# Gates of four batches computed further ahead inside a recurrence, with smaller weight buffers

## The chip, the cores and the metric

The kernel runs on one core of one Trainium2 chip. The metric is the device time of one execution in microseconds (us); lower is better. All data and matmuls are float32.

## The reference, cut to what matters

Input x has 16 batches, 512 time steps and 512 features. Four layers follow one another, each added to its input: x = x + layer(x).

```
L0: x1 = x + (x + gated wavelet)       -> the kernel uses x1 = x * (2 + gate)
L1: h_t = tanh(x1_t @ Wx + b + h_(t-1) @ Wh),  x2 = x1 + h          (512 steps, one after the other)
L2: f = sigmoid(x2 @ Wf + bf); i = sigmoid(x2 @ Wi + bi)
    s = f + i + eps;  f = f / s;  i = i / s * (x2 @ Wc + bc)
    out = scans over time of f and i;   x3 = x2 + out
L3: layer_b = base + A_b @ B_b^T  (A_b, B_b of rank 8, from cond);  out = x3 + x3 @ layer_b
```

The gates f and i and the candidate of L2 at step t need only x2 at that step. The scans need all steps.

## The kernel before, in words

There are two parts. The first is the recurrence L1: 64 blocks (index n) of T = 8 steps (index s). The order of the instructions on PE, ACT, DVE and SP is written out by hand there (a manual schedule), so program order is queue order. Features lie on partitions in four chunks of 128 (KC = 4).

In each step PE first does the recurrent matmuls (line 459, issued by `accumulate`, L320; 16 of them, four side by side in array columns of 32), from the state h of the step before. Then come other matmuls that don't depend on this step: `inputs` (L333, again through L320) of the next block, as many calls as `SHARE` (L435) says, two a step, four matmuls each; in steps 4 to 7 of blocks 0 to 16 one `factor_part` (L292), which makes the rank-8 factors of L3 from its weights; and from step 128 on one call of `early_gate` (L337, matmuls L352). Then ACT does four tanh (L485) and DVE four transposes (L486), which give the next state. In half of the steps DVE then adds x1 and h to x2 (L491), in the others it makes x1 of a later block (L158). After that `do_jobs` (L501) issues work that `later` has put off to this step. At the end of steps 7, 0 and 2 `begin` (L412) copies the bias into a bank of the next block or the one after (L428, on ACT).

`early_gate` makes L2's gates for the first TE = 128 steps of all batches. A unit is one gate (f, i or candidate) of one output chunk j of two batches: 256 columns, four calls (one for each input chunk k). After the fourth, ACT takes a sigmoid (L377), DVE does the sum (L394), the reciprocal in four parts (L380), two products (L383, L399) and the candidate (L387), spread over the next steps by `later`, and f and i are stored to the DRAM tile `early` (L374). The PSUM banks of these units alternate between `pf` and `pg`, each of one buffer; `pf` is also the bank of `factor_part`. The tiles of f, i and s are taken from the tag `w2` of six buffers of 128 x 512, which is also that of L3's weights: `load_chunks` (L257) and `load_factor` (L273) load two of a factor's four weight chunks in step 1 and two in step 6 of the block before the one that uses them. `store_factor` (L301) writes the factor to DRAM at the block's end, in four stores. After blocks 2 to 9 two chunks of the gate weights or of `base` are loaded (L512 to L516), the four matrices in turn.

All loads and stores are issued by the queue of SP, in program order.

The second part goes through the batches b (L618). `gate_unit` (L539) does one output chunk j: 12 matmuls for the steps from TE on (L544), sigmoids (L559), loads of the early gates (L558), on DVE a sum, reciprocal (L561), products and three scans (L569, L573, L575), on POOL two sums that give x3 (L578, L579). `make_layer` (L593) makes layer_b. `last_layer` (L605) of batch b runs after the second unit of batch b + 1, with 16 matmuls (L610), copies by ACT (L614) and stores (L615); for the last two batches it runs at the very end. The banks `pf`, `pi` have one buffer, `pc` two; tiles f, i, s and the output tiles two.

## Time and profile before

| | us |
|---|---|
| median of three runs (1655.62 to 1656.74) | 1656.73 |
| the profiled execution | 1657.68 |
| its span, first to last instruction | 1655.8 |
| PE busy (98% of the span) | 1627.2 |
| DVE busy (68%) | 1125.6 |
| ACT busy | 426.4 |
| POOL busy | 207.0 |

First tanh of block 8 at 131.67, of block 16 at 238.59, of block 17 at 253.63, last step at 910.79. The first gate matmul of the second part starts at 912.13.

Times in the lines shown later are microseconds from the start of the span. A line of the timeline holds start, duration, engine, source line, operation, what it writes and reads, shapes and count, and in brackets the time for which the engine was idle before it, and what ended that. PE is TensorE's matmuls, PEld its weight loads, SPq the issue of a transfer. A line of the chain of waits holds start, duration, engine and line. A line of the groups holds, after the first bar, busy time in us and mean ns of one. One matmul call of float32 appears as two records.

### The profile page before, as it was taken

What the parts mean: (1) busy time and instruction counts of PE and PEld (TensorE: products, weight loads), DVE (VectorE), ACT (ScalarE), POOL (GpSimd) and SP (SyncE); (2) the same over time, 40 slices, a digit from 0 to 9 for tenths busy, and PEclk for the clock granted to TensorE, in tenths of its full rate; (3) what the DMA queues carried; (4) which work ended last, traced back from release to release, by engine and by line L of the source; (5) the groups of instructions that cost most, each with busy time, mean ns of one, the idle gap of its engine ahead of it and who ended that gap; (6) DMA issues with size and microseconds to landing.
All of it is one profiled execution on the core that took longest, in us unless ns stands there. A gap on an engine that the chain in (4) does not pass through costs nothing.

```text
span 1655.8 us, 70230 instructions
## 1 busy us (share of the span) xinstructions
PE 1627.2 (98%) x30501; PEld 1176.0 (71%) x30501; DVE 1125.6 (68%) x3557; ACT 426.4 (26%) x2507; POOL 207.0 (12%) x209
## 2 busy tenths in 40 slices
PE   7999999999999999999999999999999999999998
PEld 6888888888888888888888555555555555555553
DVE  3445545555565555555555888889888888888985
ACT  3333333333333333333333111111111111111111
POOL 0000000000000000000000322233232222232321
PEclk9999999999999999999999999999999999999999
DMA  6344331111111111111110011110101111111001
GB/s 197 114 144 152 113 94 30 33 37 36 36 36 35 34 37 36 36 37 36 36 36 17 27 37 41 39 40 21 38 33 39 39 38 41 37 40 40 24 29 54
DMA packets 100805, 83.60 MB, mean 50 GB/s; under 512 B 10880, under 2 KB 78976, under 8 KB 100496
## 3 DMA queue, kind: packets, MB, share of 16 engines
q1 hardware_dynamic: 99392, 79.02, 15.3%
q8 instruction: 239, 3.92, 1.0%
q14 instruction: 70, 0.57, 0.1%
q10 hardware_dynamic: 1104, 0.08, 0.0%
HBM read 53.38 MB, written 25.69 MB: 48 GB/s over the span
## 4 chain that ended last, share of the span: by engine, by line
PE 93%; DVE 4%; issue 1%; ACT 1%; DMA 0%; SPq 0%; POOLq 0%; POOL 0%; DVEq 0%; ACTq 0%
PE pre L320 40%; PE po L610 12%; PE pg L352 10%; PE pf L544 9%; PE pi L544 9%; PE pc L544 9%; DVE h_out L486 1%; DVE s L561 1%; PE pl L600 1%; ACT a L485 1%; PE pf L292 1%; DVE s L569 0%; DMA w_sb<-in_w1T_dram 0%; DVE s L573 0%; DVE i L572 0%
## 5 line engine op out<-in xcount | busy, mean ns | idle before, releaser
L320 PE MATMUL pre<-wh_sb,h_out 128*32 128x128 f32 x16384 | 547.6, 273 | 10.2 <-DVE h_out L486 1.5
L320 PEld LDWEIGHTS pre<-wh_sb,h_out 128*32 128x32 f32 x16384 | 454.7, 109 | 107.4 <-DVE h_out L486 101.8
L486 DVE STREAM_TRANSPOSE h_out<-a 128x32 f32<-128x32 f32 x2048 | 262.1, 185 | 359.4 <-ACT a L485 358.4
L485 ACT ACTIVATE a<-pre 128x32 f32<-128x32 f32 x2048 | 238.2, 202 | 566.9 <-PE pre L320 564.9
L320 PE MATMUL pre<-wx_sb,x 128*32 128x128 f32 x8192 | 320.9, 273 | 1.3 <-issue 1.2
L320 PEld LDWEIGHTS pre<-wx_sb,x 128*32 128x32 f32 x8192 | 235.6, 110 | 6.9 <-ACT pre L428 4.2
L610 PE MATMUL po<-layer,x 128*128 128x512 f32 x480 | 208.4, 592 | 0.0
L544 PE MATMUL pf<-x,wf_sb 128*128 128x384 f32 x512 | 177.3, 489 | 1.0 <-DVE x L491 1.0
L544 PE MATMUL pc<-x,wc_sb 128*128 128x384 f32 x512 | 175.6, 486 | 0.0
L544 PE MATMUL pi<-x,wi_sb 128*128 128x384 f32 x512 | 175.6, 486 | 0.0
L610 PEld LDWEIGHTS po<-layer,x 128*128 128x128 f32 x480 | 91.2, 190 | 111.6 <-issue 107.6
L561 DVE RECIPROCAL s<-s 128x384 f32<-128x384 f32 x64 | 163.4, 2553 | 2.2
L544 PEld LDWEIGHTS pf<-x,wf_sb 128*128 128x128 f32 x512 | 95.9, 190 | 79.9 <-issue 18.1
L544 PEld LDWEIGHTS pi<-x,wi_sb 128*128 128x128 f32 x512 | 97.3, 190 | 67.8
L544 PEld LDWEIGHTS pc<-x,wc_sb 128*128 128x128 f32 x512 | 97.3, 190 | 67.8
L578 POOL TENSOR_TENSOR s<-s,f 128x512 f32<-128x512 f32 x64 | 87.6, 1368 | 387.4 <-DVE s L573 375.2
L491 DVE TENSOR_TENSOR x<-x,h_out 128x128 f32<-128x128 f32 x256 | 101.1, 395 | 31.9 <-PE pg L352 2.9
L533 POOL MEMSET zero<- 128x1 f32 x1 | 0.1, 99 | 912.9 <-DMA early<-ei 912.9
L559 ACT ACTIVATE f<-pf,vec_sb 128x384 f32<-128x384 f32 x64 | 37.3, 582 | 275.2 <-POOL s L578 115.0
L614 ACT COPY osb<-po 128x512 f32<-128x512 f32 x64 | 37.5, 586 | 266.2 <-PE po L610 170.0
L560 DVE SCALAR_TENSOR_TENSOR s<-f,i 128x384 f32<-128x384 f32 x64 | 36.7, 573 | 100.3 <-ACT i L559 100.3
L579 POOL TENSOR_TENSOR x<-s,x 128x512 f32<-128x512 f32 x64 | 81.4, 1272 | 5.0
(82 smaller groups left out, 1271.7 us busy)
## 6 DMA issues: line engine op xcount, KB each, us to landing
xb<-in_xT_dram SPq DMA_DIRECT2D x64, 256.0 KB
w<-in_l3w_dram SPq DMA_DIRECT2D x64, 256.0 KB
out_dram<-osb SPq DMA_DIRECT2D x64, 256.0 KB
early<-ef SPq DMA_DIRECT2D x32, 128.0 KB
early<-ei SPq DMA_DIRECT2D x32, 128.0 KB
f<-early SPq DMA_DIRECT2D x64, 64.0 KB
i<-early SPq DMA_DIRECT2D x64, 64.0 KB
w_sb<-in_w1T_dram SPq DMA_DIRECT2D x1, 1024.0 KB
```

The costliest lines, as they stand in the source:

```text
L320: nc.tensor.matmul(pre[PLACE[g][0]][j * BP : (j + 1) * BP, PLACE[g][1], :], lhsT, tile_columns(w, j), start=False, stop=False, skip_group_ ...
L352: nc.tensor.matmul(ps[c * BP : (c + 1) * BP, :, :], w[:, k, j * P + c * BP : j * P + (c + 1) * BP], x2[:, k, pair, :TE], start=(k == 0), s ...
L485: nc.scalar.activation(a[:, at], pre[bank][:, place, at], AF.Tanh)
L486: nc.vector.transpose(turned[:, c, :], a[:, at])
L491: nc.vector.tensor_tensor(x2[:, :, :, at].rearrange("p k b t -> p k t b"), xs[n][:, :, t0 // 2, :, :], turned.rearrange("p k (t b) -> p k ...
L544: nc.tensor.matmul(p[:, TE:], w_sb[:, k, j * P : (j + 1) * P], x2[:, k, b, TE:], start=(k == 0), stop=(k == KC - 1),)
L559: nc.scalar.activation(gate[:, new], p[:, new], AF.Sigmoid, bias=col(bias, j))
L561: nc.vector.reciprocal(s[:, new], s[:, new])
L578: nc.gpsimd.tensor_tensor(s, s, f, ALU.add)
L579: nc.gpsimd.tensor_tensor(x3[:, j, :], s, x2[:, j, b, :], ALU.add)
L610: nc.tensor.matmul(po, x3[:, k, at], layer[:, k, :], start=(k == 0), stop=(k == KC - 1))
L614: nc.scalar.copy(osb, po)
```

## The change

`early_gate` works on a list of parts, `PARTS`, each with its batches and steps, in place of pairs of batches with the steps 0 to 127. The list is: batches 12 to 15, steps 0 to 63; the six pairs of batches 0 to 11, steps 0 to 127; batches 12 to 15, steps 64 to 127, then 128 to 191. Each part has 256 columns. The first part's 48 calls are made in steps 64 to 127 (blocks 8 to 15), in the steps s of `SLOTS` of each block; the others from step 128 on, one a step, as before. In blocks 8 to 15 `SHARE` moves calls of `inputs`. The units of the first part, and one after it, use the bank `pg` alone; in that part the candidate is first copied by ACT with its bias to a tile `ec`. The tiles ef, ei, es, ec have one buffer each of 128 x 256. L3's weights have four buffers in place of six; a factor's first two chunks are loaded in step 6 of the block before its use, the other two in step 0 of the block that uses them, with the loads of its bias. The gate weights come matrix by matrix. In the second part, batches 12 to 15 compute the steps from 192 on and load 192.

```diff
-TE = 128
+FIRST, MAIN = 64, 128
+SLOTS = (0, 2, 4, 5, 6, 7)
+QUAD = slice(12, 16)
+PARTS = [(QUAD, slice(0, 64))]
+PARTS += [(slice(b, b + 2), slice(0, 128)) for b in range(0, 12, 2)]
+PARTS += [(QUAD, slice(64, 128)), (QUAD, slice(128, 192))]
+TE = 192
...
-            tiles.append(w2pool.tile([P, D], F32, tag="w2", name=f"{name}_{k}", bufs=6))
+            tiles.append(w2pool.tile([P, D], F32, tag="w2", name=f"{name}_{k}", bufs=4))
...
-        b, j = divmod(group, KC)
-        pair = slice(2 * b, 2 * b + 2)
+        part, j = divmod(group, KC)
+        batches, steps = PARTS[part]
+        shape = [P, batches.stop - batches.start, steps.stop - steps.start]
+        first = part == 0
+        single = first or u == 3 * KC
         if k == 0:
-            pool, tag = ((ps_p, "pf"), (ps_q, "pg"))[u % 2 if u else 1]
+            pool, tag = ((ps_p, "pf"), (ps_q, "pg"))[1 if single else u % 2]
...
-                x2[:, k, pair, :TE],
+                x2[:, k, batches, steps],
...
             early_gate.tiles = [
-                w2pool.tile([P, D], F32, tag="w2", name=f"{name}_{group}", bufs=6)[:, : 2 * TE].rearrange(
-                    "p (b t) -> p b t", b=2
-                )
-                for name in ("ef", "ei", "es")
+                w2pool.tile(shape, F32, tag=tag, name=f"{tag}_{group}") for tag in ("ef", "ei", "es", "ec")
             ]
...
-            nc.sync.dma_start(out=early[pair, which, j].rearrange("b p t -> p b t"), in_=got)
+            nc.sync.dma_start(out=early[batches, which, j, :, steps].rearrange("b p t -> p b t"), in_=got)
...
+            if first:
+                nc.vector.tensor_tensor(i, i, candidate, ALU.mult)
+            else:
+                nc.vector.scalar_tensor_tensor(i, ps, col(C_BH, j), i, ALU.add, ALU.mult)
...
+        now = early_gate.step
         if which == 0:
-            later(q if u == 0 else q + 2, lambda: sigmoid(f, C_BF))
+            later(now if single else now + 2, lambda: activate(f, AF.Sigmoid, C_BF))
...
-            later(q + 4, times_candidate)
+            if first:
+                later(now, lambda: activate(candidate, AF.Identity, C_BH))
+            later(now + (3 if first else 4), times_candidate)
...
+    SHARE = [[(2 * s, 2 * s + 2) for s in range(T)] for _ in range(NBLK)]
+    SHARE[0] = (0, 0), (0, 0), (0, 0), (0, 3), (3, 7), (7, 10), (10, 13), (13, 16)
+    for n in range(FIRST // T, MAIN // T):
+        SHARE[n] = (0, 2), (2, 6), (6, 8), (8, 12), (12, 13), (13, 14), (14, 15), (15, 16)
...
-            if n < 2 * R and s in (1, KC + 2):
-                coming = load_factor(n, coming, range(KC // 2) if s == 1 else range(KC // 2, KC))
+            if n < 2 * R and s == KC + 2:
+                coming = load_factor(n, None, range(KC // 2))
+            if 0 < n <= 2 * R and s == 0:
+                loaded = load_factor(n - 1, loaded, range(KC // 2, KC))
...
-            q = n * T + s - TE
-            if q >= 0:
-                early_gate(q)
+            step = n * T + s
+            if step >= MAIN or step >= FIRST and s in SLOTS:
+                early_gate.step = step
+                early_gate(made)
+                made += 1
...
-                k, which = divmod(i, 4)
+                which, k = divmod(i, KC)
...
+        te = TE if b in range(B)[QUAD] else MAIN
...
-                    p[:, TE:],
+                    p[:, te:],
...
-                    x2[:, k, b, TE:],
+                    x2[:, k, b, te:],
...
-        old, new = slice(0, TE), slice(TE, S)
+        old, new = slice(0, te), slice(te, S)
...
-            nc.sync.dma_start(out=gate[:, old], in_=early[b, which, j])
+            nc.sync.dma_start(out=gate[:, old], in_=early[b, which, j, :, old])
```

## The prediction

> **What bounds the kernel now.** I read the mean clock first (0.999, so no throttling to explain), then the busy slices, the timeline of single steps of the recurrence, the groups, and last the chain of waits of the end. A block is 8 steps of the recurrence, a step is the time from one first tanh (L485) to the next, a piece is one call of early_gate (4 matmuls of 256 columns).

> Blocks 1 to 15 have no gate work. One step of block 10, from the timeline:

> ```profile
> 161.09 0.65 PE L320 MATMUL pre<-wx_sb,x 128*32 128x128 f32 x16
> 161.34 0.47 ACT L485 ACTIVATE a<-pre 128x32 f32<-128x32 f32 x4 [1.18 <-PE pre L320]
> 161.57 0.59 DVE L486 STREAM_TRANSPOSE h_out<-a 128x32 f32<-128x32 f32 x4 [0.98 <-ACT a L485]
> 161.83 0.81 PEld L320 LDWEIGHTS pre<-wh_sb,h_out 128*32 128x32 f32 x32 [0.37 <-DVE h_out L486]
> 162.98 0.47 ACT L485 ACTIVATE a<-pre 128x32 f32<-128x32 f32 x4 [1.01 <-PE pre L320]
> ```

> The loop is closed: recurrent matmuls, tanh, transpose, next recurrent matmuls. Its tanhs come 1.64 us apart, and the last bracket of PEld shows 0.37 us in which PE waits for the transpose. The steps with factor matmuls (165.12 to 169.58) have the same 1.645. So the steps are bound by latency, with PE not filled. From step 128 on it is otherwise:

> ```profile
> 302.45 0.46 PEld L320 LDWEIGHTS pre<-wx_sb,x 128*32 128x32 f32 x16
> 302.80 0.47 ACT L485 ACTIVATE a<-pre 128x32 f32<-128x32 f32 x4 [1.28 <-PE pre L320]
> 302.88 0.24 PEld L352 LDWEIGHTS pg<-x,wf_sb 128*32 128x32 f32 x8
> 303.30 0.91 PEld L320 LDWEIGHTS pre<-wh_sb,h_out 128*32 128x32 f32 x32 [0.17 <-DVE h_out L486]
> 304.19 0.46 PEld L320 LDWEIGHTS pre<-wx_sb,x 128*32 128x32 f32 x16
> ```

> Weight loads start at 302.45, 302.88, 303.30, 304.19: inputs take 0.43, the gate piece 0.42, the recurrent part 0.89, together 1.74. PE is the bound here, and a step is 1.742 (301.06, 302.80, 304.55). With factor matmuls (0.22) as well, steps of block 16 are 1.96 apart (247.75, 249.71, 251.67, 253.63).

> In the second part (from 912) PE runs 24 gate records of one unit at 0.322 us each (2.575 per 8), and one batch takes 45.96 us (one reciprocal at 1543.13, the same one a batch later at 1589.10). DVE needs 9.13 us for one unit (1543.13, 1552.27, 1561.40) and idles 7.15 us a batch: PE is the bound until the last batches. There the chain of waits changes engine:

> ```profile
> 1571.31 2.58 PE pf L544 x8
> 1573.89 2.59 PE pi L544 x8
> 1576.51 0.59 ACT i L559
> 1577.19 0.57 DVE s L560
> ...
> 1634.13 1.20 DVE f L575
> ...
> 1636.53 1.26 POOL s L578
> ...
> 1639.18 13.14 PE po L610 x26
> ```

> From 1577.19 to 1636.4 the end hangs on DVE alone (six units), then POOL, while PE idles 2.6 us before the last layer.

> [...]after the idle at 1636.6 the granted clock is 0.50 from 1639.95 for 3.4 us. [...]this trace has 0.322 us at 384 and 0.431 at 512 columns, 0.85 ns a column and record, and that decides. [...]sigmoids at 256 columns 475 to 499 ns.[...]

> **Part 1, the first pieces (steps 64 to 127).** 48 pieces enter, six a block. PE per new step: steps 0 and 2: 0.89 + 0.43 + 0.42; steps 1 and 3: recurrent 0.87 and four input calls 0.87; steps 4 to 7: 0.87 + 0.22 + 0.22 + 0.43. Each is 1.74; the moved inputs make them even. 64 x (1.742 - 1.645) = +6.2 us: of 20.6 us of new matmuls (48 x 0.43) some 14 go into PE time that is idle today. The ACT sigmoids and Identity (0.5 us) run after the gate ends, 1.05 us after the recurrent part, and finish by 1.53; the next tanh is due at 1.81, so they are hidden. One exception: in odd blocks the candidate ends in step 7, and the copy of the bias into the next bank (0.38) comes behind Identity, at 1.91, while PE wants that bank at 1.74. The waits of before have this case 16 times for 4.2 us, 0.26 each; four times is +1.0. If cover is missing everywhere, the ACT job of 0.5 us is paid 12 times, 6 us. DVE gets transposes 0.49, x2 or x1 0.25 to 0.40 and one job of 0.42 to 0.53: at most 1.42 of 1.74, hidden as after step 128. The table load moves from block 16 (there it cost 2.15 - 1.74 = 0.41) to block 8: 0.

> **Part 2, single buffers for f, i, s, candidate.** A sigmoid now waits until the store of the tile's former content has landed. In the steady part f is stored four steps (7.0 us) before it is written again, and a store lands 2.0 us after issue (914.12, POOL freed 916.14): 0. Stores of 256 B pieces I take at 2 to 3 us, still 0. In block 16 the distance is three steps, and the store stands in SP's queue behind four factor stores (1.7 to 2.6), two weight loads (0.9 to 1.9) and now four bias loads (1.8 to 2.8) issued at step 0. Counted from the last tanh of block 15, it is issued after 6 to 9 us and lands at 8 to 11; the sigmoid is due at 8.1, with 0.5 of slack in such a step. Bounds 0 and +2.6; I take +0.7. Behind that ACT wait stand the tanhs. In blocks 10, 12, 14 the sigmoid is due at 11.5: 0. On SP the x load of step 3 stands behind these stores, which wait for DVE in steps 0 and 2, before it: 0.[...]

> **Part 3, four L3 buffers.** The second half of a block's weights is issued at its start instead of one block ahead, in the place of SP's queue where today the next block's first half is. In block 10 that is 161.81, behind two gate weight loads; the DMA engines move 0.95 MB from 162 to 165, so these are in at about 165.5. PE needs them in steps 6 and 7, at 168.0 and 169.6: lead 2.5 us, cost 0. The bias loads move with it, used only at the block's end: 0. The order in which gate weights come: all of f, i, candidate are in by the end of block 7: 0. With the lead gone, see rival D.

> **Part 4, the second part.** Batches 12 to 15 have 320 new columns in place of 384. PE: 64 x 0.852 = 0.0545 us a record, 24 records: 1.308 us a unit. DVE:

> ```profile
> L561 DVE RECIPROCAL s<-s 128x384 f32<-128x384 f32 x64 | 163.4, 2553 | 2.2
> L380 DVE RECIPROCAL es<-es 128x64 f32<-128x64 f32 x128 | 68.4, 535 | 0.0
> ```

> 6.31 ns a column, so 0.40; the four other operations by their rows at 384 and 256 (573/418, 555/421, 559/418, 610/469) lose 0.07 to 0.08 each: 0.69 a unit in all. The loads from DRAM grow from 64 to 96 KB[...]; DVE reads these columns 3.4 us after its unit's start: hidden. PE gains twice what DVE gains. Up to the last layer of batch 13, ten such units are on PE's path: 10 x 1.308 = -13.1, if PE does not stall. From there six units are on DVE's path: -4.1. But DVE also starts later relative to PE:

> ```profile
> 1570.07 0.32 SPq L558 DMA_DIRECT2D i<-early  x1
> 1571.41 0.32 SPq L558 DMA_DIRECT2D f<-early  x1
> 1571.78 3.24 SPq L615 DMA_DIRECT2D out_dram<-osb  x3
> 1574.08 0.59 ACT L614 COPY osb<-po 128x512 f32<-128x512 f32 x1 [5.53 <-DMA out_dram<-osb]
> ```

> SP's output stores stand behind loads that wait for DVE (scan ended 1570.04) and POOL; ACT's last copy waits for such a store, and the next sigmoids stand behind it. DVE can start its next unit no sooner than 5.7 us after its scan. Counting from the first gate matmul of each batch period: DVE has 38.81 - 4 x 0.69 = 36.05 us of work, PE's period falls to 45.96 - 5.23 = 40.73. Today DVE starts at 6.04 and ends 1.1 before the next period. After the mixed period it ends 0.13 after it and starts at 5.81; then 1.13 and 6.81; then 2.13 and 7.81. That is 1.8 later than 6.04 at the start of the tail. PE does not stall yet: its next f bank is wanted at 7.6 and free at 7.2; x3 is done at 28.9 and wanted at 29.6. So the tail gives -4.1 + 1.8 = -2.3. PE then idles about 8 us before the last layer, not 2.6; today 3.4 us of it run at half clock (1.7 lost)[...]: bounds 0 and +1.7, I take +0.9.

> **Sum.** +6.2 +1.0 +0.7 -13.1 -2.3 +0.9 = -6.6 us. Against the profiled execution (1657.68, of which the span is 1655.8): 1651.1. The median of the runs shown is 0.95 below that execution: 1656.73 - 6.6 = 1650.1.

> **Rivals.** A, as above, 1650.1, within 1647.5 to 1653. B, no drift: SP's chain doesn't push DVE, the tail gives 4.1, the clock costs nothing more, block 16 doesn't wait: -6.6 - 1.8 - 0.9 - 0.7 = -10.0, 1646.7. For it: start and end of DVE are computed on lags of under 2 us. C, the gain is mostly lost: steps cost 1.79 (the first of block 16 did: 238.59 to 240.38), 64 x 0.05 = 3.2, and the store in block 16 comes at its worst, +1.9: -1.5, 1655.2. D, slower: the second half of L3's weights is late. The lead of 2.5 us rests on two gate loads and three stores ahead of it; if these loads land over 2.5 us later than today's rate says, PE waits in step 6 of every block with factors. At 1 us beyond that point, 16 blocks cost 16 us: -6.6 + 16 = +9.4, 1666. Against it: the rate is seen in this very window. That the change doesn't do what it says is excluded: the order of instructions has the 48 pieces and matmuls of 320 columns.

> **Numbers.** A 0.55, B 0.20, C 0.14, D 0.11. About 0.2% (3.3 us) is what a measurement of this kernel tells from no change. Faster: A and B, 0.75; same: C, 0.14; slower: D, 0.11. Range: from 1645.5 (B with a shorter block part) to 1655.5 (C).

> **What would show it.** Right: tanhs 1.74 apart in blocks 8 to 15; the start of the second part 7 to 9 us later; gate records of 320 columns at 0.267 us; DVE's idle gap a batch shrinking from 7.15 us to about 5.7; PE idle for about 8 us before its last layer. Wrong: waits of PE for DMA in steps 6 and 7, tanhs over 1.8 apart, PE waiting for ACT between batches 12 and 14, or an idle under 4 us at the end.

## The result, and the profile after

The changed kernel takes 1656.13 us (median, 1652.66 to 1657.46) beside 1656.7 for the kernel before. The medians are 0.6 us apart; the ratio over all runs is 0.9989 with a 95% interval of 0.9982 to 0.9997, some 1.8 us less. Measured once more, as the control of a later group of experiments, the ratio was 0.9999 (0.9990 to 1.0007). So the two ratios put what the change brings between nothing and two microseconds, and their intervals reach from 1.2 us lost to 3.0 us gained. The forecast was 6.6 less, 1650.1. The median, 1656.13, lies 0.6 above the upper end of the range; the ratio, taken on the forecast's own base of 1656.73, gives 1654.9, which is 0.6 inside it. The forecast's sign is no more than half right, its size is wrong.

The span of the profiled execution (1656.13) is 1654.2 us, beside 1655.8. Cut into stages, by the first tanh of each block (L485 before, L508 after) and the last of all:

| stage | before, us | after, us | change | forecast |
|---|---|---|---|---|
| start to block 8 | 131.67 | 132.09 | +0.4 | 0 |
| blocks 8 to 15 | 106.93 | 117.66 | +10.7 | +7.2 |
| block 16 | 15.04 | 16.49 | +1.5 | +0.7 |
| block 17 to last step | 657.15 | 656.60 | -0.6 | 0 |
| last step to end | 745.06 | 731.34 | -13.7 | -14.5 |

The second part did nearly what was forecast. What was lost was lost in blocks 8 to 16, and the page does not show it at first: PE is at 98% of the span as before, and its waits for other engines are small. So I listed the time of each single step. In blocks 8 to 15 most tanhs are 1.74 or 1.75 us apart, as forecast. But 14 of the 64 steps are late, by 0.1 to 0.9 us, together 6.1 us. (Late is what a step takes over 1.742, or over 1.645 where no gates are made, counted above 0.04.) The kernel before has 1.7 us of this in these blocks. One such step, step 3 of block 9 (steps are counted from 0), from the timeline of the changed kernel:

```profile
151.88 0.47 ACT L508 ACTIVATE a<-pre 128x32 f32<-128x32 f32 x4 [0.23 <-PE pre L328]
...
152.40 0.46 PEld L328 LDWEIGHTS pre<-wh_sb,h_out 128*32 128x32 f32 x16
...
152.79 0.42 DVE L406 SCALAR_TENSOR_TENSOR es<-ef,ei 128x256 f32<-128x256 f32 x1
153.59 0.71 PE L328 MATMUL pre<-wh_sb,h_out 128*32 128x128 f32 x17 [0.47 <-issue]
153.59 0.43 PEld L328 LDWEIGHTS pre<-wh_sb,h_out 128*32 128x32 f32 x16 [0.73 <-DVE es L406]
...
154.33 0.47 ACT L508 ACTIVATE a<-pre 128x32 f32<-128x32 f32 x4 [1.98 <-PE pre L328]
```

PE's weight loads stop at 152.86 in the middle of the 32 recurrent matmuls of one step, after 16 of them, and go on 0.73 us later; the next tanh comes 2.45 after the last. The bracket of PEld names DVE's es, but a recurrent matmul reads nothing of es, and PE's own bracket says "issue": it waited for nothing that the profile shows. All waits of PE in blocks 8 to 15, and those of its weight loads:

```profile
PE pre L328 <- issue: 2.4, 5, 0.7
PE pf L300 <- issue: 0.4, 1, 0.4
...
PEld pre L328 <- DVE h_out L509: 3.8, 22, 0.2
PEld pre L328 <- issue: 3.2, 5, 0.9
PEld pf L300 <- issue: 1.0, 2, 0.7
PEld pre L328 <- ACT pre L443: 1.0, 4, 0.2
```

The columns are the total, the number and the longest. In the kernel before the line that answers to the first is one wait of 0.7, and PEld's wait for the transpose (L486 there) is 17.4 us, 60 times. That is the idle PE time which the pieces were to fill, and they filled it: 3.8 are left. The wait for the bias copy (L443) is there four times, as forecast. The waits for "issue" have grown: in the kernel before PEld has two of them, 1.2 us.

Then block 16. Its step 3 took 3.45 us:

```profile
255.32 0.39 SPq L382 DMA_DIRECT2D early<-ef  x1
...
255.80 1.34 SPq L382 DMA_DIRECT2D early<-ei  x1
...
258.27 0.47 ACT L385 ACTIVATE ef<-pg,vec_sb 128x256 f32<-128x256 f32 x1 [2.62 <-DMA early<-ef]
258.64 0.45 ACT L508 ACTIVATE a<-pre 128x32 f32<-128x32 f32 x4
258.79 0.16 PEld L364 LDWEIGHTS pg<-x,wi_sb 128*32 128x32 f32 x8 [1.55 <-ACT ef L385]
```

The store of f is issued at 255.32, and the sigmoid that writes f's only tile again starts at 258.27, after an idle of 2.62: the landing took 2.9 us. The tanhs stand behind it on ACT. This is the wait that the forecast named, at 1.7 us rather than 0.7.

In the second part the 320-column reciprocal, PE's waits, and DVE's first operation after its idle gap in batches 12, 13 and 14 are, from the groups, the waits and the timeline:

```profile
L585 DVE RECIPROCAL s<-s 128x320 f32<-128x320 f32 x16 | 34.4, 2153 | 0.5
...
L588 DVE TENSOR_TENSOR i<-i,s 128x320 f32<-128x320 f32 x16 | 8.7, 546 | 0.0
L586 DVE TENSOR_TENSOR f<-f,s 128x320 f32<-128x320 f32 x16 | 8.7, 541 | 0.4
```

```profile
PE po L634 <- POOL x L603: 3.9, 1, 3.9
PE pf L568 <- ACT f L583: 2.6, 2, 1.8
PE po L634 <- DVE base_sb L627: 1.1, 1, 1.1
```

```profile
1494.65 0.49 DVE L584 SCALAR_TENSOR_TENSOR s<-f,i 128x320 f32<-128x320 f32 x1 [5.67 <-ACT i L583]
...
1537.06 0.49 DVE L584 SCALAR_TENSOR_TENSOR s<-f,i 128x320 f32<-128x320 f32 x1 [5.51 <-ACT i L583]
...
1579.23 0.49 DVE L584 SCALAR_TENSOR_TENSOR s<-f,i 128x320 f32<-128x320 f32 x1 [5.56 <-ACT i L583]
```

The gap is 5.5 to 5.7 us, where 5.7 was the forecast. PE's unit before the gap's end began at 1488.65, 1529.49 and 1570.70, so DVE starts 6.0, 7.6 and 8.5 us behind PE, where 5.81, 6.81 and 7.81 were forecast: the drift is there and somewhat larger. PE idles 3.9 us ahead of the last layer, not 8; the lines show another 3.7 us for which it stood for ACT and DVE shortly before.

### The profile page after: what moved, and what is told of

Same layout as the page of the kernel before. It is cut to its first block, busy times and chain, and to the rows that moved or that the text cites. A ratio compares the mean times of both kernels' runs of the same rounds, so it can differ in the third digit from the quotient of the medians.

```text
span 1654.2 us, 71063 instructions
## 1 busy us (share of the span) xinstructions
PE 1621.6 (98%) x30885; PEld 1193.3 (72%) x30885; DVE 1126.9 (68%) x3589; ACT 428.3 (26%) x2519; POOL 206.3 (12%) x209
## 3 DMA queue, kind: packets, MB, share of 16 engines
q8 instruction: 242, 3.96, 1.1%
## 4 chain that ended last, share of the span: by engine, by line
PE 94%; DVE 3%; issue 1%; ACT 1%; DMA 1%; SPq 0%; POOLq 0%; POOL 0%; DVEq 0%; ACTq 0%
PE pre L328 41%; PE po L634 12%; PE pg L364 11%; PE pf L568 9%; PE pi L568 9%; PE pc L568 9%; PE pl L624 1%; PE pf L300 1%; DVE s L585 1%; DVE h_out L509 1%; ACT a L508 1%; DVE s L593 0%; DMA w_sb<-in_w1T_dram 0%; DVE s L597 0%; DVE i L596 0%
## 5 line engine op out<-in xcount | busy, mean ns | idle before, releaser
L328 PE MATMUL pre<-wh_sb,h_out 128*32 128x128 f32 x16384 | 553.3, 273 | 8.1 <-issue 2.1
L328 PEld LDWEIGHTS pre<-wh_sb,h_out 128*32 128x32 f32 x16384 | 462.4, 110 | 100.6 <-DVE h_out L509 86.2
L508 ACT ACTIVATE a<-pre 128x32 f32<-128x32 f32 x2048 | 238.0, 203 | 566.6 <-PE pre L328 564.0
L328 PEld LDWEIGHTS pre<-wx_sb,x 128*32 128x32 f32 x8192 | 240.3, 110 | 6.6 <-ACT pre L443 5.1
L568 PE MATMUL pf<-x,wf_sb 128*128 128x384 f32 (+1 forms) x512 | 170.6, 476 | 3.5 <-ACT f L583 2.6
L568 PE MATMUL pi<-x,wi_sb 128*128 128x384 f32 (+1 forms) x512 | 168.8, 473 | 0.0
L568 PE MATMUL pc<-x,wc_sb 128*128 128x384 f32 (+1 forms) x512 | 168.8, 473 | 0.0
L585 DVE RECIPROCAL s<-s 128x384 f32<-128x384 f32 (+1 forms) x64 | 157.0, 2453 | 2.2
L583 ACT ACTIVATE f<-pf,vec_sb 128x384 f32<-128x384 f32 (+1 forms) x64 | 36.4, 568 | 280.3 <-POOL s L602 134.7
L584 DVE SCALAR_TENSOR_TENSOR s<-f,i 128x384 f32<-128x384 f32 (+1 forms) x64 | 35.5, 555 | 95.3 <-ACT i L583 95.3
L364 PE MATMUL pg<-x,wi_sb 128*32 128x256 f32 x1152 | 90.6, 379 | 1.3 <-ACT ef L385 1.3
```

What stands on the lines that cost most here:

```text
L328: nc.tensor.matmul(pre[PLACE[g][0]][j * BP : (j + 1) * BP, PLACE[g][1], :], lhsT, tile_columns(w, j), start=False, stop=False, skip_group_ ...
L364: nc.tensor.matmul(ps[c * BP : (c + 1) * BP, :, :], w[:, k, j * P + c * BP : j * P + (c + 1) * BP], x2[:, k, batches, steps], start=(k == ...
L508: nc.scalar.activation(a[:, at], pre[bank][:, place, at], AF.Tanh)
L568: nc.tensor.matmul(p[:, te:], w_sb[:, k, j * P : (j + 1) * P], x2[:, k, b, te:], start=(k == 0), stop=(k == KC - 1),)
L583: nc.scalar.activation(gate[:, new], p[:, new], AF.Sigmoid, bias=col(bias, j))
L584: nc.vector.scalar_tensor_tensor(s[:, new], f[:, new], EPS, i[:, new], ALU.add, ALU.add)
```

## The experiments

**What stops PE.** The page counts 61,770 PE instructions (30,885 matmuls and as many weight loads), and in its list of DMA queues:

```profile
q8 instruction: 242, 3.96, 1.1%
```

That is 242 packets of 16 KB, and 3.96 MB over 61,770 is 64 bytes for one PE instruction: I read queue 8 as bringing PE's program, 256 instructions a packet, while the kernel runs. With the 159 semaphore and drain instructions that the trace records on PE's queue there are 61,929, and 242 packets hold 61,952; the kernel before has 61,165 and 239 packets for 61,184. If PE stops because its next instructions are not there, all its stops must stand at one and the same place modulo 256. I numbered all recorded instructions of PE's queue, those for semaphores too, and looked up the packet of queue 8 that started last before PE went on. All idles of PE's weight loads over 0.45 us in blocks 7 to 16:

```
idle of PE, us        its place in the      last packet    PE goes on after   next packet,
                      program, modulo 256   of queue 8     the packet's start us after that
128.99 - 129.53       193                   126.72         2.81               1.10
140.69 - 141.37       193                   138.93         2.44               1.05
152.86 - 153.59       194                   151.32         2.27               1.20
169.23 - 170.16       194                   167.96         2.21               1.19
181.77 - 182.60       193                   180.27         2.32               1.23
214.30 - 215.06       193                   212.26         2.81               1.09
234.77 - 235.25       194                   233.03         2.22               1.23
257.24 - 258.79        94                   255.72         3.07               2.34
```

The first seven stand at one place modulo 256, 193 or 194. The eighth is the wait for f's sigmoid, and stands elsewhere. Why the place is 193 and not 0 is not shown. The six in blocks 8 to 15 sum to 4.4 us, beside 6.1 us of late steps there. It is the same everywhere: in the thirteen profiles of this document all 75 idles over 0.45 us in blocks 0 to 62 that are labelled "issue" stand at 193 or 194, those of the kernel before included.

After each of the seven the next packet starts 1.05 to 1.23 us later, which I read as a fetch one packet ahead. In the seven, PE goes on 2.21 to 2.81 us after a packet's start. I take the shortest, 2.2 us, as what a packet needs, an estimate from these seven: a packet must then start at least 2.2 us before PE is through with the one before. In blocks 8 to 15 of the changed kernel a block has 928 PE instructions in 13.94 us of even steps, so 256 last 3.84 us, and a packet may start up to some 1.6 us after PE has begun the one before. In this profile it starts 1.2 us after that (median of the 29 packets of blocks 8 to 15, up to 2.6), and 0.6 us (28 packets, up to 1.6) in blocks 17 to 24. What is open so far is why a packet starts late. Theory F: since the DMA engines are full of weights. Its rival is theory O: the late steps come of the new order of work. The next two kernels take these loads away, and add them where none are.

**Taking the loads away.** This kernel leaves out the weights of 15 of the 16 factors, so its last layer is not the one of the reference; the matmuls stay.

```diff
+    kept = []
     def load_factor(i, loaded, ks):
...
-            loaded = [], bias, ps_p.tile([P, P], F32, tag="pf", name=f"pf_{i}")
+            loaded = kept, bias, ps_p.tile([P, P], F32, tag="pf", name=f"pf_{i}")
         w, bias, _ = loaded
-        load_chunks(w, l3w2[which, r], f"w2_{i}", ks)
+        if i == 0:
+            load_chunks(w, l3w2[which, r], f"w2_{i}", ks)
```

> This kernel is the changed one, with the weights of L3's first factor loaded once and used for all 16 factors (so 15 of 16 weight loads, 15 MB in blocks 1 to 15, are left out; matmuls, bias loads and stores stay). In the changed kernel 64 even steps of 1.742 would give 111.5 us for blocks 8 to 15, and 117.7 were measured, 6.2 of it in some 15 single late steps. Theory F (instruction fetch): these late steps are PE waiting for its own instructions, which come over the DMA engines and are late where these are full of L3's weights; then blocks 8 to 15 fall to about 112.8 (table load 0.4 and the copies behind Identity 0.7 stay), blocks 1 to 7 from 94.8 to about 92.3, block 16 keeps at least part of its 1.7 us wait, and the time falls by 7 to 9 us, to about 1648. Theory O (the new order itself: Identity and sigmoid ahead of tanhs, uneven input calls, DVE jobs): blocks 8 to 15 stay at 117 to 118, and the time falls by at most 2.

Blocks 1 to 7 fell to 92.43 us (late steps 0.4 instead of 2.8), blocks 8 to 15 to 113.61, 0.8 above what theory F said and 3.4 below what O allows. PE's waits in blocks 8 to 15 of this kernel:

```profile
PE pre L331 <- issue: 0.3, 1, 0.3
...
PEld pre L331 <- ACT pre L446: 1.0, 4, 0.3
PEld pre L331 <- issue: 0.6, 2, 0.4
PEld pg L367 <- ACT ef L388: 0.5, 1, 0.5
```

Of PEld's 4.2 us for "issue", 0.6 are left, and of the 2.1 us of late steps 1.0 are the waits for the bias copy and the table load (0.41, in step 5 of block 8). A packet now starts 0.7 us after PE has begun the one before (median), not 1.2. The share of the 16 DMA engines that the data take in these blocks fell:

```profile
q1 hardware_dynamic: 15232, 13.57, 39.5%
```

```profile
q1 hardware_dynamic: 10624, 5.18, 16.9%
```

(the changed kernel first, then this one; packets, MB, share). The time fell by less than expected: 1651.35, ratio 0.9959 (0.9946 to 0.9973), 5 us under the changed kernel's first ratio, not 7 to 9. Block 16 still had its wait (step 3 took 3.63), and the end cost 1.3 more.

**Adding them where there are none.** Blocks 17 to 24 have nothing but loads of x and stores of gates, 112 PE instructions a step. The changed kernel has 1.0 us of late steps there: three behind a copy of the bias, 0.2 each, which every kernel here has, and one of 0.4.

```diff
+            if 2 * R < n <= 3 * R and s in (0, KC + 2):
+                tiles = load_chunks(tiles if s else [], l3w2[1, n - 2 * R - 1], ...)
```

> This kernel is the changed one, with the weights of eight L3 factors (8 MB) loaded once more in blocks 17 to 24, at the places in the blocks where blocks 8 to 15 have them; nothing reads them. These blocks have the same 112 PE instructions a step as blocks 8 to 15, took 112.5 us, and have no late step. Theory F: late steps appear as in blocks 8 to 15, some 4 to 6 us in all (116.5 to 118.5 for blocks 17 to 24), PE's idle before them with no instruction named that it waits for; the time rises to about 1661. Theory O: loads that nobody reads cost nothing, 112.3 to 113, the time within 0.5 of the changed kernel's.

Blocks 17 to 24 took 115.4 us instead of 112.5: late steps of 3.9 us instead of 1.0. The 2.9 more are under the 4 to 6 expected. PE's waits from 268 to 382 us, nearly the whole of these blocks:

```profile
PE pre L328 <- issue: 1.5, 3, 0.8
...
PEld pre L328 <- DVE h_out L512: 5.2, 29, 0.3
PEld pre L328 <- issue: 2.5, 4, 1.1
PEld pre L328 <- ACT pre L443: 0.7, 3, 0.3
```

All four idles over 0.45 us in these blocks (the fourth ends at 382.84) stand at the place of the others, 193 or 194 modulo 256, and PE goes on 2.26 to 3.15 us after a packet's start. A packet starts 1.15 us (median) after PE has begun the one before, where it was 0.6. Loads that nothing waits for and nothing reads stop PE: theory F holds, and O falls. The time was 1662.01, ratio 1.0026 (1.0016 to 1.0036), some 6 us over the changed kernel, of which these blocks explain 2.9. In the profile, which is of the slowest of the nine runs, what it has over the changed kernel's profile lies, beside the 2.9, for the most part in block 16 (2.6) and behind the last step (1.6), where the edit changes nothing; why none of the nine runs is under 1660.6 stays open. The wait in block 16 came at 3.5 us there, and PE's clock fell with it:

```profile
258.00:260.00 2.00, 0.34 (x14) 0.07 (x4) 0.00 (x0) 0.00 (x0) 0.00 (x0) 1.00 0.38 82
260.00:262.00 2.00, 1.46 (x28) 1.25 (x32) 0.86 (x5) 0.82 (x5) 0.00 (x0) 0.74 0.41 120
262.00:264.00 2.00, 2.00 (x44) 2.00 (x40) 0.49 (x4) 0.47 (x4) 0.00 (x0) 0.50 0.04 8
```

(stretches of 2 us; the third number from the end is the granted clock, 1.00 for full speed). After an idle of 2.2 us PE ran at half clock (0.50 from 262 to 264), and steps 4 and 5 of block 16 took 2.6 and 2.7.

**Is it the later loads (part 3)?** The kernel before with part 3 alone (f, i and s have tiles of their own for it, in lines not shown).

```diff
-            tiles.append(w2pool.tile([P, D], F32, tag="w2", name=f"{name}_{k}", bufs=6))
+            tiles.append(w2pool.tile([P, D], F32, tag="w2", name=f"{name}_{k}", bufs=4))
...
-            if n < 2 * R and s in (1, KC + 2):
-                coming = load_factor(n, coming, range(KC // 2) if s == 1 else range(KC // 2, KC))
+            if n < 2 * R and s == KC + 2:
+                coming = load_factor(n, None, range(KC // 2))
+            if 0 < n <= 2 * R and s == 0:
+                loaded = load_factor(n - 1, loaded, range(KC // 2, KC))
```

> This kernel is the one before, with part 3 of the change alone: four buffers for L3's weights, the second half of a factor's weights issued at the start of the block that uses them; f has two tiles of its own, i and s one each, so that no store of f is waited for in block 16. Theory F (late steps come of a full DMA and a dense instruction stream, not of when a load is issued): the late steps of blocks 1 to 15, 3.6 us in the kernel before, stay between 2.5 and 5, no step waits for a weight, the time within 1.5 us of before. Rival L (the later loads are what brings the late steps): they rise to 7 or more, the time by 3 to 5.

1657.41, ratio 0.9997 (0.9988 to 1.0005): no change. Late steps were 3.2 in blocks 1 to 7 and 2.8 in 8 to 15, 6.0 in all, above the 5 that was expected and under the 7 of the rival. How much of that is chance is told by the kernel before, profiled again:

> This is the kernel before once more, for the sum of its late steps in one more execution: 2.0 us in blocks 1 to 7 and 1.7 in blocks 8 to 15 in the first profile. Theory F with density (96 PE instructions in 1.645 us leave a fetch more room than 112 in 1.742): 1 to 3 us in blocks 8 to 15 again, under the 4.3 to 6.2 of the changed kernel's profiles. Rival (chance between executions): anything up to 6.

It had 2.4 and 2.8, 5.3 in all. So part 3 costs nothing that these runs can tell.

**How much the late steps scatter.** The changed kernel again:

> This is the changed kernel itself once more, beside the three below on the same chip. All theories: within 0.2% of the first measurement, 0.997 to 1.000 of before; what its late steps sum to in blocks 8 to 15 tells how much they scatter between executions (6.2 us in the first; I expect 4 to 8).

Ratio 0.9999 (0.9990 to 1.0007), late steps in blocks 8 to 15 of 4.3 us in this profile. Five profiles have these blocks unchanged (this, the first, and three kernels of below): 117.7, 115.8, 117.8, 117.7 and 117.4, mean 117.3. The two of the kernel before give 106.9 and 108.1, mean 107.5. The blocks cost 9.8 us, 2.6 more than forecast.

**The wait in block 16.** After block 15 the candidate's tile is idle, and f can use it in turn.

```diff
-                w2pool.tile(shape, F32, tag=tag, ...) for tag in ("ef", "ei", "es", "ec")
+                w2pool.tile(shape, F32, tag=tag, ...)
+                for tag in (("ef", "ei", "es", "ec") if first else (("ec", "ef")[group % 2], "ei", "es"))
```

> This kernel is the changed one, with f of every second group after block 15 in the tile of the candidate, which is idle from there on. Theory S (the 1.7 us of step 3 of block 16 are the sigmoid waiting for the landing of the store of the same tile, issued 1.6 us before): step 3 of block 16 falls from 3.45 to 1.74, block 16 from 16.5 to 14.8, the time by 1.7 to about 1654.4. Rival: the next single tile, i, or the queue behind the stores takes the wait over: block 16 stays above 16, the time within 0.5 of the changed kernel's.

Step 3 of block 16 took 1.80, block 16 15.01 (16.49 and 16.19 in the changed kernel's two profiles), and ACT has no wait for a DMA there any more. So theory S is shown by the trace. The time, 1655.76, ratio 0.9988 (0.9980 to 0.9995), does not show it: 1.5 us is less than the late steps scatter.

**The drift at the end.** Output stores issued by ACT.

```diff
-            nc.sync.dma_start(out=out[b, at, :], in_=osb)
+            nc.scalar.dma_start(out=out[b, at, :], in_=osb)
```

> This kernel is the changed one, with the 64 output stores of the second part issued by ACT, behind the copy that fills their tile, and no longer by SP, where they stand behind loads that wait for DVE and POOL. Theory Q (DVE's late start, 5.9, 7.5 and 8.5 us after PE's start in batches 12, 13 and 14, comes through SP's queue): DVE's idle gaps of 5.6, 5.5 and 5.5 us in these batches shrink to under 4, the six units of the end start up to 2.5 us sooner, the time falls by 1.5 to 2.5, to about 1654. Rival P (DVE starts late since PE hands over late or since ACT's copies stand ahead of its sigmoids on ACT itself): gaps stay over 5 us, the time within 0.5.

1653.88, ratio 0.9974 (0.9966 to 0.9982). DVE after its gap, in this kernel:

```profile
1494.56 0.49 DVE L584 SCALAR_TENSOR_TENSOR s<-f,i 128x320 f32<-128x320 f32 x1 [4.80 <-ACT i L583]
...
1535.40 0.49 DVE L584 SCALAR_TENSOR_TENSOR s<-f,i 128x320 f32<-128x320 f32 x1 [4.17 <-ACT i L583]
...
1576.25 0.49 DVE L584 SCALAR_TENSOR_TENSOR s<-f,i 128x320 f32<-128x320 f32 x1 [4.18 <-ACT i L583]
```

The gaps are 4.1 to 4.8 (a little over the 4 expected), and DVE starts 5.1 us behind PE in all three batches instead of 6.0, 7.6 and 8.5. The part from the last step to the end took 729.0 instead of 731.3. Theory Q holds: the drift came through SP's queue. In this execution the wait for f's store also came once in block 10 (2.3 us, ACT idle), where the forecast had said 0.

**Both, and more.** The two edits together:

> This kernel is the changed one with the edits of the second f tile and of the output stores on ACT together. Theories S and Q both: the wait of 1.7 in block 16 and 2.3 of the tail are at different places and add up, -3.5 to -4.5 us from the changed kernel, 0.9955 to 0.997 of before. Rival: what is gained in block 16 is lost in the scatter of the late steps, no more than -2.5.

1652.42, ratio 0.9968 (0.9957 to 0.9980), 5.1 us under its control on the same chip, a little more than expected. Then L3's loads one a step, alone and with both edits, and the base weights' loads moved out of these blocks:

```diff
-            if n < 2 * R and s == KC + 2:
-                coming = load_factor(n, None, range(KC // 2))
+            if n < 2 * R and s > KC:
+                coming = load_factor(n, coming, range(s - KC - 1, s - KC))
             if 0 < n <= 2 * R and s == 0:
-                loaded = load_factor(n - 1, loaded, range(KC // 2, KC))
+                loaded = load_factor(n - 1, loaded, range(KC - 1, KC))
...
-        for i in (2 * n - 4, 2 * n - 3):
+        for i in (2 * n - 4, 2 * n - 3) if n < T else (2 * n - 28, 2 * n - 27) if n >= 20 else ():
...
-        if n == 2 * KC + 4:
+        if n == 6 * KC:
```

(the first hunk in all three kernels below, the other two in the last alone)

> This kernel is the changed one, with L3's four weight loads of a block issued in steps 5, 6, 7 and 0, each as soon as its buffer is free, and no longer two in step 6 and two in step 0. Theory F with a load on the DMA engines as such: as many microseconds of full DMA, late steps as before, 5 to 8 us in blocks 8 to 15, the time within 1 us of the changed kernel's. Theory F with the burst (an instruction fetch waits for all that is queued ahead of it): half as long a queue, the late steps fall to 2 to 4 us, and the time by 2 to 4.

> This kernel is the changed one with the second f tile, the output stores on ACT and the weight loads one a step. The first two gave 0.9968 of before together. If the single loads are worth the 2 us that they seemed to give alone (0.9987 beside 0.9999), 0.995 to 0.9963; if that was scatter, as the late steps of its profile say (7.7 us, not fewer), 0.9963 to 0.9975.

> This kernel is the one of all three edits, with the four base weight loads (1 MB) moved from the ends of blocks 8 and 9 to those of blocks 20 and 21, where no other weights are loaded. Theory F: late steps of blocks 8 and 9 (1.3 us in the first profile of the changed kernel, 0.4 of it the table load) fall to about 0.8, none appear in blocks 20 to 22, the time within 1 us of the kernel beside it; a gain of 1.5 or more would say that the loads of a whole block before weigh on its fetches.

One a step alone: 0.9987 (0.9978 to 0.9995), its control 0.9999, so 2 us less if the medians are taken at their word; but its profile has 7.7 us of late steps in blocks 8 to 15, not the 2 to 4 of the burst theory; that a fetch waits for all that is queued ahead of it is not shown. With both edits 1651.13, 0.9958 (0.9944 to 0.9971), late steps of 7.6 us. With the base weights later 1649.91, 0.9956 (0.9944 to 0.9969), late steps 3.9, in blocks 20 to 22 none but the one behind the bias copy; blocks 8 and 9 kept 1.6 us of theirs, twice what was expected. The two times are the same within their intervals. Whether single loads gain anything stays open: the medians say so, the late steps of the profiles do not. The version of all these edits beats the kernel before by 0.4% and the changed one as well.

## Why the prediction was right and wrong, by its own steps

That the result lies at the upper end of the range, just in or just out, is no success of its mechanism. That end was set for rival C, with dearer steps throughout. The late steps that took most of the gain were in neither the sum nor a rival.

- **PE's even steps, +6.2: right.** The steps of blocks 8 to 15 that are not late are 1.74 to 1.77 apart, with 1.742 in the middle, and PE's idle before the transposes is filled. The ACT and DVE jobs are hidden, as said.
- **The copy behind Identity, +1.0: right.** Step 0 of blocks 10, 12, 14 and 16 is 0.2 to 0.28 late, and the wait is listed four times, 1.0 us; the steps pay about 0.9. The table load (1283 ns) moved as said, 0.41 in block 8. The copies with Identity brought no further one: the trace has four table loads, as before.
- **"The steps are bound by latency" and "Each is 1.74": the step that failed.** The sum took the even step for all 64 steps. The kernel before has late steps too, and in plain sight: steps of 2.63 and 2.64 us in blocks 5 and 10, 1.7 to 2.8 us in blocks 8 to 15. The forecast did not ask what they were. Both hold a stop of PE at place 193, 0.87 and 1.01 us long. By that place they are PE's own instruction fetch behind weight loads, and the change makes the room for it smaller: a block of the kernel before has 832 PE instructions in 13.16 us of even time, so 256 last 4.05 us, and now 3.84. With the 2.2 us that I take a packet to need, it may start 1.85 us after PE has begun the one before, and now 1.64. (The expectations' 96 and 112 a step leave out the factor matmuls and the moved inputs; on average it is 104 and 116.) The late steps rose from 1.7 and 2.8 to 4.3 to 6.2, of which 1.1 are three of the copies and the table load, and in some profiles a part is a wait for f's store. That the loads cause them is shown, by taking them away and by adding them. That the smaller room is why they grew is argued from these counts, and from the packets' starts in blocks 8 to 15, which are alike: in the two profiles of each kernel they come 1.15 us (before, 52 packets) and 1.23 us (changed, 58) after PE has begun the packet before, in the median, and nine in ten within 2.0. No run changed the count of instructions alone.
- **The store in block 16, +0.7 with bounds 0 and +2.6: mechanism right, size off.** It measured 1.7 in the first profile, 1.4 to 2.6 in other profiles with the same code in block 16, since the landing took 2.9 us and more. The last such store, also in pieces of 256 B, took 2.0 us (926.18, POOL freed 928.17), as the last one of the kernel before did. The second tile takes it away. The zero for blocks 10, 12 and 14 was too sure: four of the ten profiles of the changed kernel and its variants have one such wait in block 10 or 12, of 0.6 to 2.3 us.
- **Four buffers, 0: right,** shown by part 3 alone (0.9997). Rival D is out: in no profile does PE wait for a weight of L3 in steps 6 and 7.
- **PE's path in the second part, -13.1: right.** From PE's first gate matmul of batch 12 to that of batch 13 it is 40.84 us, forecast 40.73; the next is 40.93. Counted from the first gate matmul of the second part to that of the third unit of batch 14, PE gained 12.4 us.
- **DVE's path at the end, -4.1 + 1.8 = -2.3: both terms off.** Reciprocals gave 0.40 a unit as said and the two operations with a bias or EPS 0.07 each. The two products gave 0.01 each instead of 0.07 (541 and 546 ns beside 554 and 551), so a unit gained 0.56, not 0.69, and six units 0.8 less. The mean hides two kinds: 20 of these 32 products took 476 to 492 ns, which is the gain that was forecast, and 12 took 594 to 747. Each of the 12 overlaps one of POOL's sums, as do only four of the 20; that POOL is the cause is not shown. The drift was 2.5, not 1.8. Its mechanism is shown: without SP's queue in the way the end is 2.3 us shorter.
- **Half clock at the end, +0.9: wrong premise.** PE idled 3.9 us, not 8, as it had waited 2.6 us for f's sigmoid and 1.1 for the last layer's base in batch 15, which the forecast excluded ("PE does not stall yet"). The 26 matmuls after it took as long as before in this pair, 12.97 us beside 13.12. They scatter: 11.4 to 13.1 us in three profiles with the old end (one of them without half clock), 12.9 to 14.5 in ten with the new one. Their means, 12.5 and 13.6, are 1.1 apart, so the size came out after all, and on another idle than the one forecast: luck. The bounds, 0 and +1.7, were my estimate: the one stretch at half clock that I had seen was 3.4 us long, after an idle of 2.6. After the 3.9 us of the changed kernel it is 3.4 us as well, from 1637.4.

Rival C came closest: it had the result's size, and the store of block 16 at its worst. But its other half, 1.79 for each step, was not what happened: the steps stayed at 1.74, and a few were late.

## What to carry to other kernels

List the time of every repeat of a loop, not its typical value: the few that are longer may be a limit of their own, and filling the loop's idle time may feed it (1.7 and 2.8 us of late steps became 4.3 to 6.2 here). Where an engine has "issue" waits in the middle of a run of equal instructions, count its place in the program, semaphore instructions included, and take the remainder by the size of an instruction packet (256 here). Before counting on idle PE time next to bulk loads, compare the time that one packet of instructions lasts (3.84 us in blocks 8 to 15 of the changed kernel) with the time from one packet's start to its use (2.21 us or more in the stops there).
